# Keeping the turned context of the first cross attention in DRAM for the keys of the second

## The chip, the cores and the metric

The kernel runs on one core of a Trainium2 chip. The metric is the device time of one execution in microseconds (us), of which the median of several runs is taken. A profiled execution gives, beside its own time, a record of each instruction and transfer. The engines are PE (TensorE, matrix products; its weight loads are recorded apart as PEld), DVE (VectorE), ACT (ScalarE), POOL (GpSimd) and SP (SyncE, which here issues transfers). SBUF is the memory on the core that the engines work on; PSUM holds the results of matrix products; DRAM is reached by DMA.

## The reference

A perceiver block with six residual stages: `x` has 16 batches of 64 latents of 256 features, the context has 16 batches of 1024 tokens of 256 features.

```python
x = x + L0_xattn(layernorm(x), ctx_1024)      # first cross attention, raw context
x = x + L0_attn(layernorm(x))
x = x + L0_ffn(layernorm(x))
x = x + L1_xattn(ctx_1024, layernorm(x))      # second cross attention
x = x + L1_attn(layernorm(x))
x = x + L1_ffn(layernorm(x))                  # routed experts
```

The second cross attention matters here. It normalises the context itself, with a gain and a shift, and turns the keys by a rotary embedding over the token's position:

```python
xn = (x - mean(x)) * rsqrt(var(x) + EPS) * gamma_x + beta_x
k_x, v_x = split(xn @ Wkv)           # 8 heads of 64
k_x = k_x * cos + neg_half(k_x) * sin
sim = q @ concat(k_x, k_l).T
out = (softmax(sim) @ concat(v_x, v_l)) @ Wo
```

`k_l` and `v_l` come from the 64 latents of the batch. All arithmetic is in float32.

## The kernel before

**Three stages.** Everything is in one program. The first stage (main loop at L697, 128 steps) does the first cross attention, 16 batches by 8 pairs of heads; the small stages after it (self attention and feed-forward, `small_stages` L307) are cut into pieces and woven in between. The second (main loop at L1434, 64 steps, from about 1153 us to 1982 us) does the second cross attention, with the self attention and the routing of the last stage woven in. The third runs the experts.

**First stage.** A batch's context is loaded in two halves of 512 tokens (`load_ctx` L216, 512 KB each, issued on SP into the pool of context buffers). The scores need the context with features on the partitions: `turn_context` (L552) turns it with transposes on DVE and 16 copies from SBUF to SBUF into `ctxT[b]`, two buffers of 128 x 2 x 1024 elements. The first batch is turned on PE (`first_context` L540). The tokens of `ctxT` stand in blocks: the index is (a, k, s), token 128 k + 32 a + s. `context_stats` (L571) gathers mean and variance of each token into `cstat`. Softmax probabilities are turned by one DVE transpose (`x_pb`, L606) and 16 copies on SP (`x_pT`, L612); the products with the context (`x_po`) take them. `x_out` is the last product of the stage.

**Second stage.** For each half of 512 tokens: `fetch` (L804) loads the raw context again, up to four halves ahead; `normalise` (L809) subtracts the mean and multiplies by 1/std in place, on ACT, a quarter (256 tokens) at a time; `turn_context` (L821) turns a quarter with four transposes on PE (`l_pt`, issued by line 105) and evicts them in two ACT instructions that multiply by the gain (L835) into `l_cnT`. `keys` (L857) makes keys (a "key pair" is two calls of it, for four of the eight heads): four matmuls (`l_pk`), two evictions on ACT with the bias (L877, `l_kr`), a product with cos on DVE (L878), four copies on SP that swap halves (L886, `l_ks`), a product with sin on POOL (L889) and a sum on DVE (L890). `gather` (L1052) multiplies the probabilities with the normalised context not turned (`l_po`); it has one PSUM buffer, emptied on DVE (L1066, `l_pct`). Probabilities are turned as in the first stage (L1019, 16 copies `l_pT` at L1028). `shifts` (L844) makes the bias of keys and values from the layer norm's shift, in 32 narrow matmuls (`l_pb`).

**What orders the work.** In the second stage PE keeps the order in which the program writes its matrix instructions. The other engines' order is set by a scheduler from that text, the dependencies and the buffers. Each engine works its own list in order, so what stands behind a waiting instruction waits too. `weave` (L1407) interleaves keys, turning, the woven pieces (`items`) with the eight products of `gather` for the step (`fill`). At the head of the stage (from L1388) the statistics of the latents, the first normalisations, `shifts`, the first turnings and four key pairs run in the order written, then the main loop starts. All small PSUM results (`l_pt`, `l_pk`, `l_pb` and those of the woven stages) share a pool of three banks.

## Time and profile before

| | |
|---|---|
| runs | 2128.99, 2125.99 and 2124.79 us, median 2125.99 |
| profiled execution | 2112.25 us, its span from first to last instruction 2110.5 us |
| mean granted TensorE clock | 0.990 |
| busy | PE 2021.1, DVE 1313.3, ACT 816.8, POOL 342.0 us |
| DMA | 225.82 MB, mean 107 GB/s |
| bias of keys (`l_pb`) | 3.68 us, at 1152.96 us |
| turning (`l_pt`, `l_cnT`) | 256 transposes on PE, 128 evictions on ACT |
| sin products (L889) | 128 on POOL, 166.2 us, mean 1319 ns |

How it is read: the profile gives each engine's busy time and the number of its instructions; a table of stretches gives the same for parts of the span, with the granted clock and the busy share of the DMA engines. A group's row names a line, an engine and an operation with its tiles (`out<-in`), the count, and the shortest, median and longest duration in ns. A waits' row names an instruction, what released it, and how long in total, how often and how long at most it waited. The timeline lists groups of instructions by start and duration. A float32 matrix product leaves two records, a transpose one. Many steps share helper lines: 101 is every matmul, 105 every transpose by PE, so tiles tell them apart.

### The profile page before, as it was taken

Reading aid. Unit: us, or ns where it says so; the run is one execution under the profiler, and the core shown is the slowest. Engines: PE = TensorE matmul, PEld = TensorE weight load, DVE = VectorE, ACT = ScalarE, POOL = GpSimd, SP = SyncE. Lnnn points to the kernel's source line nnn. Section 1 sums busy time; section 2 is a strip of 40 time slices with the busy share of each in tenths; the row PEclk is TensorE's granted clock in tenths of the full one; section 3 lists DMA queues with packets and bytes.
Section 4 is the critical chain, followed back from the end, with each engine's and each line's share of the span. In section 5 each row is a group of like instructions: output and inputs, shape, how many; then the busy total and the mean of one; then the engine's idle time right before and its main releaser. Section 6 shows DMA issues by size and latency. Waiting matters only on the chain. (4 is left out here: it accounts for less than half of the span.)

```text
span 2110.5 us, 30756 instructions
## 1 busy us (share of the span) xinstructions
PE 2021.1 (96%) x10906; PEld 1369.8 (65%) x10906; DVE 1313.3 (62%) x2678; ACT 816.8 (39%) x1584; POOL 342.0 (16%) x329
## 2 busy tenths in 40 slices
PE   7899999999999999999998889899999999999988
PEld 4567666666667666666666445566666666666777
DVE  6765656757666567576653666666767676767431
ACT  2323234224333342243343435445555545554231
POOL 3200100001001000010010323222323232323111
PEclk9999999999999999999999999999999999999999
DMA  7344334333343343344433145744444444444443
GB/s 258 86 105 103 74 83 104 98 71 99 85 105 76 83 105 98 71 116 107 109 80 90 42 98 155 202 100 111 108 105 111 109 108 105 107 101 106 132 165 109
DMA packets 159432, 225.82 MB, mean 107 GB/s; under 512 B 36408, under 2 KB 95374, under 8 KB 158768
## 3 DMA queue, kind: packets, MB, share of 16 engines
q1 hardware_dynamic: 153456, 204.12, 38.0%
q0 software_dynamic: 5824, 19.74, 2.8%
q8 instruction: 88, 1.44, 0.3%
q14 instruction: 64, 0.52, 0.1%
HBM read 71.14 MB, written 6.05 MB: 37 GB/s over the span
## 5 line engine op out<-in xcount | busy, mean ns | idle before, releaser
L101 PE MATMUL x_s<-ctxT,x_qk 128*128 128x512 f32 x1024 | 471.2, 601 | 11.5 <-ACT pr_x L597 11.5
L101 PE MATMUL x_po<-x_pT,ctx 128*128 128x256 f32 x2048 | 458.0, 381 | 3.7 <-DMA x_pT<-x_pb 3.7
L101 PEld LDWEIGHTS x_po<-x_pT,ctx 128*128 128x128 f32 x2048 | 387.6, 191 | 79.3 <-issue 26.3
L101 PEld LDWEIGHTS x_s<-ctxT,x_qk 128*128 128x128 f32 x1024 | 187.0, 190 | 211.0 <-issue 181.2
L590 DVE TENSOR_REDUCE nmax_x<-x_s 128x1 f32<-128x1024 f32 x128 | 155.9, 1218 | 238.7 <-PE x_s L101 237.6
L597 ACT ACTIVATE pr_x<-x_s,shift_x 128x1024 f32<-128x1024 f32 x128 | 142.5, 1114 | 287.8 <-DVE shift_x L594 239.5
L101 PE MATMUL l_po<-l_pT,l_ctx 128*128 128x256 f32 x864 | 239.3, 390 | 14.0 <-DMA l_ks<-l_kr 5.8
L101 PE MATMUL l_pk<-l_cnT,wkv 128*128 128x512 f32 x512 | 243.5, 602 | 2.9 <-DVE a_vm L369 1.5
L889 POOL TENSOR_TENSOR l_ks<-l_ks,k 128x512 f32<-128x512 f32 x128 | 166.2, 1319 | 402.3 <-DMA l_ks<-l_kr 338.9
L101 PEld LDWEIGHTS l_po<-l_pT,l_ctx 128*128 128x128 f32 x864 | 154.4, 194 | 83.7 <-issue 61.9
L606 DVE STREAM_TRANSPOSE x_pb<-pr_x 128x1024 f32<-128x1024 f32 x128 | 157.2, 1237 | 6.3 <-DMA x_pT<-x_pb 2.1
L101 PEld LDWEIGHTS l_pk<-l_cnT,wkv 128*128 128x128 f32 x512 | 94.8, 191 | 101.5 <-issue 85.1
L877 ACT ACTIVATE l_kr<-l_pk,l_bkv 128x512 f32<-128x512 f32 x128 | 87.3, 686 | 184.2 <-PE l_pk L101 106.0
L631 ACT COPY x_pct<-x_po 128x512 f32<-128x512 f32 x64 | 37.5, 585 | 244.6 <-PE x_po L101 244.6
L878 DVE TENSOR_TENSOR l_kT<-l_kr,k 128x512 f32<-128x512 f32 x128 | 91.8, 719 | 46.5 <-ACT l_kr L877 46.2
L190 DVE TENSOR_SCALAR pr_x<-pr_x,inv_x 128x1024 f32<-128x1024 f32 x128 | 100.1, 782 | 3.2
L890 DVE TENSOR_TENSOR l_kT<-l_kT,l_ks 128x512 f32<-128x512 f32 x128 | 95.3, 784 | 8.2 <-POOL l_ks L889 8.1
L996 DVE TENSOR_REDUCE nmax_l<-l_s 128x1 f32<-128x1024 f32 x64 | 75.7, 1219 | 33.9 <-PE l_s L101 33.9
L597 ACT ACT_TABLE_LOAD x42 | 53.9, 1283 | 103.9 <-DVE shift_x L594 103.8
L1019 DVE STREAM_TRANSPOSE l_pb<-pr_l 128x1024 f32<-128x1024 f32 x64 | 78.3, 1233 | 4.7 <-DMA l_ks<-l_kr 3.3
L999 ACT ACTIVATE pr_l<-l_s,nmax_l 128x1024 f32<-128x1024 f32 x64 | 71.5, 1118 | 9.8 <-DVE nmax_l L997 9.6
L101 PE MATMUL l_s<-l_kT,l_qT 64*64 64x512 f32 x512 | 66.4, 604 | 4.2 <-DVE l_kT L890 4.2
(307 smaller groups left out, 2598.5 us busy)
## 6 DMA issues: line engine op xcount, KB each, us to landing
x_pT<-x_pb SPq DMA_DIRECT2D x1024, 64.0 KB, 2.0
l_ks<-l_kr SPq DMA_DIRECT2D x256, 128.0 KB, 2.3
l_pT<-l_pb SPq DMA_DIRECT2D x512, 64.0 KB, 2.0
ctx<-in_context_dram SPq DMA_DIRECT2D x32, 512.0 KB, 5.5
w<-in_m_w_dram SPq DMA_DIRECT2D x16, 1024.0 KB, 9.8
ctxT<-x_cb SPq DMA_DIRECT2D x240, 64.0 KB, 2.0
l_ctx<-in_context_dram SPq DMA_DIRECT2D x27, 512.0 KB, 4.5
l_ctx_spare<-in_context_dram SPq DMA_DIRECT2D x5, 512.0 KB
```

What stands on the lines that cost most here:

```text
L101: ins = nc.tensor.matmul(*args, **kwargs)
L190: nc.vector.tensor_scalar(pr, pr, inv, None, ALU.mult)
L590: nc.vector.tensor_reduce(nmax, sc, AX.X, ALU.max, negate=True)
L597: nc.scalar.activation(pr, sc, AF.Exp, bias=shift, scale=1.0, accum_out=total)
L606: nc.vector.transpose(blocks[w][:, :, i], pr.rearrange("p (j k s) -> p j k s", j=4, s=32))
L877: nc.scalar.activation(kr[:, i % 2], pk, AF.Identity, bias=bkv[:, i : i + 1])
L878: nc.vector.tensor_tensor(kr2, kr[:, i % 2], k4[:, 0, at], ALU.mult)
L889: nc.gpsimd.tensor_tensor(ks[:, i % 2], ks[:, i % 2], k4[:, 1, at], ALU.mult)
L890: nc.vector.tensor_tensor(kr2, kr2, ks[:, i % 2], ALU.add)
L996: nc.vector.tensor_reduce(nmax, sc[h], AX.X, ALU.max, negate=True)
L999: nc.scalar.activation(pr[h], sc[h], AF.Exp, bias=nmax, scale=1.0, accum_out=total[:, 2 * h : 2 * h + 1])
L1019: nc.vector.transpose(blocks[w][:, :, h].rearrange("p j k s -> p k j s"), pr[h].rearrange("p (k j s) -> p k j s", k=NKT, s=32),)
```

## The change

The first stage already turns the raw context. Its result is now written to DRAM (`keep_turned`, two transfers of 512 KB a batch, on SP) and read by the second stage in place of the turning there (`load_turned`, 512 KB for each half). The raw turned context is not yet normalised. Three things take the place of that: the gain and the mean are taken into the weights of the keys (`gain_weights`, `center_weights`: each column of the weights gets its mean over the features subtracted, found with a product with ones); 1/std of each token, which now lies along the free axis, is written to DRAM as rows (`store_rstd`), read back to all partitions (`load_rstd`, 256 KB for each half) and multiplied in on POOL (`scale_turned`). `shifts` moves into the first stage's last steps. The PE transposes and ACT evictions of the second stage go.

The raw context is still loaded and normalised for `gather`, from four fixed buffers, one step ahead of its normalisation. Since the turned tokens are in blocks (a, k, s), the table of cos and sin, and the way that the probabilities are turned, follow that order. At the head of the second stage the order of key pairs and woven pieces is written anew, with four key pairs ahead of the first scores. The constant of ones, before part of a loaded table, is filled by POOL at the start.

```diff
+    def keep_turned(b, c):
+        if c == 0:
+            turned[b] = mdram.tile([P, NC, N], F32, tag=f"turned{b}", name=f"turned_{b}")
+        nc.sync.dma_start(
+            out=turned[b][:, c], in_=ctxT[b][:, c].rearrange("p a k s -> p (a k s)")
+        )
...
+    def load_turned(hh, slot):
+
+        b, n = divmod(hh, 2)
+        cn[hh] = slot.rearrange("p t d -> p (t d)").rearrange("p (c m) -> p c m", c=NC)
+        nc.sync.dma_start(out=cn[hh], in_=turned[b][:, :, n * 512 : (n + 1) * 512])
+
+    def store_rstd():
+
+        pt = bank([P, P], "l_rt")
+        transpose(pt, crstd, ident)
+        stage = slots[1][:, 0, 0:P]
+        nc.vector.tensor_copy(stage, pt)
+        for a in range(4):
+            nc.gpsimd.dma_start(
+                out=rstd_rows[:, a], in_=stage[:, 32 * a : 32 * a + 32]
+            )
...
+    def load_rstd(hh):
+        b, n = divmod(hh, 2)
+        row = rstd_rows.rearrange("b a k s -> b (a k s)")[b : b + 1, n * 512 : (n + 1) * 512]
+        nc.sync.dma_start(out=row_of(hh), in_=row.broadcast_to([P, 512]))
+
+    def scale_turned(hh):
+        nc.gpsimd.tensor_tensor(
+            cn[hh], cn[hh], row_of(hh).unsqueeze(1).broadcast_to([P, NC, 512]), ALU.mult
+        )
+
+    def gain_weights():
...
+            nc.scalar.activation(
+                w[:, c, :], wkv4[:, c, 0:512], AF.Copy, scale=cols[:, C_GX + c : C_GX + c + 1]
+            )
+        return w
+
+    def center_weights(w, pm, c):
+        nc.vector.scalar_tensor_tensor(w[:, c, :], pm, -1.0 / D, w[:, c, :], ALU.mult, ALU.add)
...
+        if i == 6:
+            keep_turned(b, 0)
+        if i == 0 and b:
+            keep_turned(b - 1, 1)
...
+        if s == NSTEP - 5:
+            store_rstd()
+            wkc = gain_weights()
+        elif s == NSTEP - 4:
+            pm = bank([P, 512], "l_wm")
+            for c in range(NC):
+                matmul(pm, lhsT=ones, rhs=wkc[:, c, :], start=(c == 0), stop=(c == NC - 1))
+            center_weights(wkc, pm, 0)
+            center_weights(wkc, pm, 1)
+            for hh in range(2):
+                load_rstd(hh)
+        elif s == NSTEP - 3:
+            shifts()
+        elif s == NSTEP - 2:
+            for hh in range(2):
+                scale_turned(hh)
...
+        raw_slots = [slots[4], slots[5], slots[0], slots[2]]
+
         def fetch(hh):
-            if hh not in raw and hh < NHALF:
-                b, h = divmod(hh, 2)
-                raw[hh] = load_half(cpool, b, h, "l_ctx", spare[:, 0] if hh % 7 == 3 else None)
+            if hh < NHALF:
+                raw[hh] = load_half(None, hh // 2, hh % 2, "l_ctx", raw_slots[hh % 4])
...
-        def turn_context(qq):
...
+        def next_turned(hh):
+            if hh < NHALF:
+                slot = spare[:, 0]
+                if hh % 3 != 1:
+                    slot = two.tile([P, 4, D], F32, tag="cnT", name=f"l_cnT_{hh}")
+                load_turned(hh, slot)
+                load_rstd(hh)
...
-                        pk, lhsT=wkv4[:, c, i * P : (i + 1) * P], rhs=cnT[hh][:, c, :],
+                        pk, lhsT=wkc[:, c, i * P : (i + 1) * P], rhs=cn[hh][:, c, :],
...
             nc.vector.transpose(
-                blocks[w][:, :, h].rearrange("p j k s -> p k j s"),
-                pr[h].rearrange("p (k j s) -> p k j s", k=NKT, s=32),
+                blocks[w][:, :, h], pr[h].rearrange("p (j k s) -> p j k s", j=4, s=32)
             )
...
+        for hh in range(2):
+            next_turned(hh + 2)
+            fetch(hh)
+        latent_stats(0)
+        latents(0)
         key_pair(0)
         issue_one()
         key_pair(2)
-        turn_context(4)
-        turn_context(5)
+        turn_latents(0)
+        queries(0)
         issue_one()
         key_pair(1)
+        issue_one()
+        key_pair(3)
         scores(0)
         soften(0, 0)
-        issue_one()
-        key_pair(3)
-        turn_context(6)
+        scale_turned(2)
+        next_turned(4)
         issue_one()
         key_pair(4)
+        for qq in range(2):
+            normalise(qq)
         for s in range(NSTEP):
             t, at = divmod(s, PER_TILE)
             if s % 2 == 0:
-                fetch((s + 8) // 2)
+                fetch((s + 2) // 2)
             elif s + 1 < NSTEP:
                 scores((s + 1) // 2)
             turn_probs(s)
             if s + 1 < NSTEP:
                 soften((s + 1) // 2, (s + 1) % 2)
-            normalise(s + 7)
+            if s % 2:
+                normalise(s + 1)
+                normalise(s + 2)
+                next_turned((s + 9) // 2)
+            elif (s + 6) // 2 < NHALF:
+                scale_turned((s + 6) // 2)
             items = [lambda j=j: keys(s + 5, j) for j in range(2)]
-            items.append(lambda: turn_context(s + 7))
```

## The prediction

> **What bounds the kernel now.** I read the totals first, then the table of busy time by stretch, then the groups of the changed lines, then the waits, and for single costs the timeline.
>
> ```profile
> PE 2021.1 (96%) x10906; PEld 1369.8 (65%) x10906; DVE 1313.3 (62%) x2678; ACT 816.8 (39%) x1584; POOL 342.0 (16%) x329
> ```
>
> TensorE (PE) is the bound over the whole span: work taken off it shortens the kernel unless another engine turns late. The stretches (columns: window, PE, PEld, DVE, ACT, POOL busy, clock, DMA share, GB/s) show where this holds less well:
>
> ```profile
> 1153.00:1170.00 17.00, 15.15 (x93) 12.77 (x92) 4.65 (x14) 11.00 (x26) 1.64 (x2) 0.80 0.21 75
> 1170.00:1190.00 20.00, 14.90 (x71) 7.99 (x69) 9.87 (x16) 8.06 (x17) 10.36 (x9) 1.00 0.23 52
> 1190.00:1240.00 50.00, 37.64 (x157) 18.13 (x161) 37.37 (x62) 19.30 (x42) 15.25 (x12) 0.90 0.34 81
> 1300.00:1500.00 200.00, 187.87 (x1092) 124.88 (x1093) 134.45 (x254) 94.49 (x202) 53.19 (x47) 0.98 0.52 138
> ```
>
> From 1153 us the second cross attention starts up: PE is idle for 87 - 67.7 = 19.3 us until 1240. After that it is 94 to 98% busy. So there are two regimes: a start that is a chain of dependent steps, and a steady part in which PE time is the time.
>
> **The change, part by part.** *Removed: the turning of the normalised context.* 64 quarters, each with 4 PE transposes, 2 ScalarE evictions and a PSUM bank.
>
> ```profile
> L105 PE MATMUL l_pt<-ident,l_ctx x216: 272/273/456, 1156.5 to 1885.5; 128*128 128x128 f32 x108
> L835 ACT ACTIVATE l_cnT<-l_pt,cols x128: 458/474/512, 1157.6 to 1916.8; 128x256 f32<-128x256 f32 x128
> L878 DVE TENSOR_TENSOR l_kT<-l_kr,k x128: 639/686/1540, 1169.4 to 1934.0; 128x512 f32<-128x512 f32 x128
> ```
> ```profile
> L270 POOL TENSOR_TENSOR x_prod<-wq,rowsb x2: 2347/2360/2372, 14.5 to 44.9; 128x1024 f32<-128x1024 f32 x2
> ```
> ```profile
> 1510.31 0.60 PE L105 MATMUL l_pt<-ident,l_ctx 128*128 128x128 f32 x4
> ...
> 1510.75 1.03 PE L101 MATMUL l_po<-l_pT,l_ctx 128*128 128x256 f32 x4
> ...
> 1516.22 2.49 POOL L889 TENSOR_TENSOR l_ks<-l_ks,k 128x512 f32<-128x512 f32 x2 [1.46 <-DMA l_ks<-l_kr]
> ...
> 1517.72 1.54 DVE L878 TENSOR_TENSOR l_kT<-l_kr,k 128x512 f32<-128x512 f32 x1 [0.22 <-ACT l_kr L877]
> ```
>
> The transpose row's 0.273 us each is not what one displaces, since matmuls overlap: 256 x 0.273 = 70 us is too much. In the timeline the next group starts 0.44 us after a group of four, so a quarter costs 0.44 us, 64 of them 28 us. The union of their busy spans (0.60 us, 64 times) gives 38 us as the other end. I take 0.43, being start to start in a full PE. 16 of the 64 quarters fall into the start-up and the steps just after it; the other 48 are worth 48 x 0.43 = **-20.6 us** (to -28 at the 0.60 of the busy spans). ScalarE loses 128 x 0.474 = 61 us; at 39% busy this is worth nothing itself, but l_k evictions find ScalarE and the three PSUM banks free sooner.
>
> *Start-up.* Now the first key matmul (l_pk) waits for normalised context, turned, evicted, and for the 32 narrow matmuls of the bias (l_pb):
>
> ```profile
> 1152.96 3.68 PE L101 MATMUL l_pb<-cols,wkv 128*128 128x1 f32 x32
> 1156.50 1.95 PE L105 MATMUL l_pt<-ident,l_ctx 128*128 128x128 f32 x8
> ...
> 1166.76 3.60 PE L101 MATMUL l_pk<-l_cnT,wkv 128*128 128x512 f32 x8
> ...
> 1187.79 1.09 PE L101 MATMUL l_s<-l_kT,l_qT 64*64 64x512 f32 x8
> ```
>
> With the change the turned keys of two halves lie ready, scaled, before 1153, so l_pk starts there. Ahead of the first scores go 3.68 (l_pb) and 1.95 + 1.91 + 1.04 = 4.9 us of transposes; one more key pair (3.6) is put ahead of them, out of what followed. The idle of 1.85 us at 1160, for the latents' statistics, is covered by l_pk. The pair is work that later steps no longer do, so 3.7 + 4.9 = 8.6 us is what the start gains if nothing else changes. I take **-8 us**, with ends -2 (the sin/cos chain through four copies, POOL and DVE becomes the limit; new waits, below) and -14 (its idle goes too).
>
> *Added on PE, in the first stage:* the bias (3.68 us by its row, only moved), two 128x512 ones-matmuls for the mean (the l_pk row has four of that size, two records each, in 3.60 us: 1.8) and one transpose of 1/std (0.1), in a stretch where PE is full (18.89 of 23.00 us before 1153): **+5.5**. ScalarE's two gains of weights, DVE's two centrings of 128x512 and the POOL copies of 1/std lie beside it. A `ones` fill put early on POOL delays the first weight load: **+0.5**.
>
> *Added on DMA.* First stage: 32 writes of 512 KB on SP. Their cost lies between 0 and what they delay. A 512 KB load took
>
> ```profile
> l_ks<-l_kr SPq DMA_DIRECT2D x256, 128.0 KB, 2.3
> ...
> l_ctx<-in_context_dram SPq DMA_DIRECT2D x27, 512.0 KB, 4.5
> ```
>
> 4.5 us to land against 2.0 for a 64 KB x_pT, so about 2.5 us behind each. They stand ahead of batches of 16 x_pT copies, mostly one or two, late in the stage up to four together: 4 x 2.5 = 10 us. The x_pT copies have 3 to 15 us from the last issue to first use (2.0 of it landing), and SP was idle 5 to 9 us before those batches. Four or so places could lose up to 3 us: 0 to 12; I take **+1**. Second stage: each half (512 tokens, 25 us) issues a turned load of 512 KB and a 256 KB broadcast of 1/std on SP, 27 issues where there were 25. The DMA share was 0.43 to 0.52, and 768 KB more on about 2.7 MB a half leaves room. The raw half now comes one step (11.4 us) before its normalisation instead of several; 4.5 to 5.5 us of landing fits. Should it not, the softmax exponent stands behind it on ScalarE, and scores behind that.
>
> *Added on POOL.* 32 products 128x1024. The nearest row is x_prod, same shape and operation: 2.36 us; 75 us in all. By half: 2.36 us more on an engine that is 27% busy here. It holds no result up while it has three steps (34 us), which it has. What it costs is the port to SBUF. The row: L878 takes 686 ns at the median and up to 1540; the one at 1517.72 took 1.54 us while POOL's pair ran from 1516.22 to 1518.71. The rule: the Trainium skill, "SBUF — State Buffer", section "Who interferes with whom", says whoever issues first gets the shared pair "for the whole instruction; the other **fully blocks**", and that DVE operations with two SBUF inputs count. By the rule at its full price each product may stop DVE for 2.36 us, and 75 us against the gain would make the sum positive (+53). The trace agrees on the blocking but not on the price to PE: in 1300 to 1880 POOL's l_ks products already hold 51 pairs x 2.5 = 128 us, while PE's whole idle, of every cause, is 21 us. So at most 16% of it reaches PE: 75 x 0.16 = 12. With l_pct, which frees the single buffer l_po, among DVE's blockable operations, I take **+3** for ports and queues, ends 0 and 12.
>
> *No cost:* the probabilities transposed in another order (DVE's 128x1024 transposes took 1233 ns in one order in L1019 and 1237 in the other in L606).
>
> **Sum:** -20.6 - 8 + 5.5 + 0.5 + 1 + 3 = **-18.6 us**. Against the profiled execution, 2112.25 us (span 2110.5, the rest around it), that is 2093.7. The runs' median is 13.7 us higher; a saved PE microsecond is the same in both, so 2125.99 - 18.6 = **2107.4 us**. Ends by the same terms: -28 - 14 + 6 = -36, 2090; -20.6 - 2 + 6 + 12 + 12 = +7, 2133. All of the worst together being unlikely, the likeliest's own range is 2092 to 2121.
>
> **Rivals.** (a) *The port takes it back.* For: POOL and DVE overlap already as shown. Against: the 21 us of idle. With +12 to +18 instead of +3 the time is 2116 to 2123, hardly a change.
>
> (b) *The key chain becomes the bound, slower.* A key pair goes ScalarE, SP's four copies, POOL, DVE, then scores.
>
> ```profile
> POOL l_ks L889 <- DMA l_ks<-l_kr: 338.9, 47, 12.0
> ```
> ```profile
> SPq L886 <- ACT l_kr L877: 70.4, 31, 17.4
> ```
>
> (What was waited for, us in total, times, longest.) POOL's idle already ends on these copies, 47 times. In the trace the chain of a pair has 3.5 to 10.7 us of slack before its scores in the steady part, and none up to about 1355 us. The new load and the broadcast are issued directly ahead of four such copies: 2.5 + 1.3 us by the landing times; and a product on POOL ahead of l_ks 2.4: 6.2 in all. It decides once the delay exceeds 3.5. At the full price (6.2 - 3.5) x 28 halves + 6.2 x 4 = 100 us; if a third of that happens, 2107 + 33 = **2140**. Against: products and loads are issued once a half, two key pairs have 25 us between them, and the three rarely meet.
>
> (c) *The writes in the first stage stall x_po.* 12 to 25 us if each late batch finds its ring full: 2118 to 2132.
>
> (d) *PE has holes where the transposes lay, so that little is gained.* Only in the start-up does the table show such holes; then only the steady 20 us minus costs remain: 2113.
>
> **How the numbers follow.** What a measurement of this kernel can tell from no change is about 0.2%, 4.3 us: 2121.7 to 2130.2. Likeliest, (d) with it, 2092 to 2121: 0.56, all faster. A larger gain, below 2092: 0.05. (a): 0.14, of it 0.05 faster, 0.07 same, 0.02 slower. (b): 0.17, slower. (c): 0.08, of it 0.02 same, 0.06 slower. Faster 0.66, same 0.09, slower 0.25. For 8 in 10: 0.04 lies below 2088, and some 0.11 above 2145, the upper two thirds of (b): **2088 to 2145**.
>
> **What would show it.** Right: no l_pt and l_cnT groups; PE busy down by some 30 us; first l_pk near 1159 (1153 and the 5.5 added before it), first l_s near 1187 with a key pair more done by then, first l_po near 1231 where it was 1233; PE at 94 to 98% in the same stretches; x_po's idle <-DMA near its 3.7. Wrong if l_s or l_pk idles on DVE l_kT or POOL l_ks by tens of us (b), if L878 and L890 have a mean near 0.9 us and l_po waits on l_pct (a), if x_po waits for x_pT by over 15 us (c), or if the first l_po comes later than 1237 (start-up).

## The result and the profile after

The changed kernel takes **2151.09 us** (median of four runs, 2147.68 to 2152.47) where the kernel before took 2125.39 (2124.75 to 2128.99): a ratio of **1.0115** with a 95% interval of 1.0097 to 1.0133. It is 25.7 us slower; 2107.4 was forecast. The profiled execution took 2151.67 us, its span 2149.8 us, at a mean granted clock of 0.975 (0.990 before). The totals, and five groups of instructions (the columns are busy time and mean ns of one, then the idle time of the engine before them and what ended it):

```profile
PE 2022.4 (94%) x10655; PEld 1358.3 (63%) x10655; DVE 1379.8 (64%) x2681; ACT 771.5 (36%) x1458; POOL 431.7 (20%) x366
```
```profile
L103 PE MATMUL x_po<-x_pT,ctx 128*128 128x256 f32 x2048 | 457.6, 381 | 5.8 <-DMA x_pT<-x_pb 5.8
...
L103 PE MATMUL l_po<-l_pT,l_slot 128*128 128x256 f32 x1024 | 280.4, 397 | 27.3 <-DMA l_pT<-l_pb 10.4
...
L948 DVE TENSOR_TENSOR l_kT<-l_kr,k 128x512 f32<-128x512 f32 x128 | 117.0, 918 | 63.2 <-ACT l_kr L947 63.1
...
L960 DVE TENSOR_TENSOR l_kT<-l_kT,l_ks 128x512 f32<-128x512 f32 x128 | 106.8, 874 | 32.8 <-POOL l_ks L959 32.6
...
L103 PE MATMUL l_s<-l_kT,l_qT 64*64 64x512 f32 x512 | 73.6, 621 | 14.1 <-DVE l_kT L960 12.3
```

PE has 251 recorded instructions fewer, and is busy for 1.3 us *more*. What the change adds on PE (two products with ones and one transpose) is small against that, so what remains takes longer. And PE idles more: 27.3 us before `l_po`, 14.1 before `l_s`. `x_po` hardly waits for its transfers (5.8 us), so the writes of the first stage aren't where the time went. L948 and L960, the product with cos and the sum on DVE, are 0.2 and 0.1 us longer than before (719 and 784 ns). The same four stretches as before:

```profile
1153.00:1170.00 17.00, 13.32 (x60) 10.41 (x61) 3.88 (x15) 3.33 (x8) 1.69 (x3) 0.90 0.39 117
1170.00:1190.00 20.00, 15.41 (x75) 10.10 (x74) 11.26 (x18) 7.76 (x17) 11.27 (x8) 0.91 0.62 190
1190.00:1240.00 50.00, 36.14 (x128) 13.61 (x126) 37.81 (x63) 23.99 (x52) 20.31 (x17) 0.90 0.38 98
1300.00:1500.00 200.00, 179.76 (x963) 114.65 (x962) 145.32 (x234) 81.83 (x165) 70.11 (x51) 0.94 0.62 167
```

In 1300 to 1500 PE is busy 179.76 of 200 us where it was 187.87, DVE is busier (145.32 against 134.45), POOL too (70.11 against 53.19), and the clock is 0.94 against 0.98. The steady part shows it best. First the kernel before, then the changed one, one row of 500 us each (PE, PEld, DVE, ACT, POOL busy, clock, DMA share, GB/s):

```profile
1400.00:1900.00 500.00, 489.53 (x3158) 324.95 (x3156) 351.48 (x699) 257.45 (x535) 134.08 (x110) 1.00 0.42 106
```
```profile
1400.00:1900.00 500.00, 468.89 (x2896) 305.62 (x2895) 388.87 (x671) 222.61 (x442) 185.84 (x126) 0.97 0.51 133
```

PE is busy for 20.6 us less of the 500, and at a clock 0.03 lower, which is another 15 us of full-speed work.

**Stage by stage**, from the same traces (us; "steady" runs from the first `l_s` of scores 8 to that of scores 30, 22 of the 32):

| | first stage ends (`x_out`) | from there to scores 8 | steady | rest |
|---|---|---|---|---|
| before | 1153.1 | 233.9 | 552.2 | 171.3 |
| after | 1168.6 | 232.9 | 572.9 | 175.4 |
| forecast of the difference | +7 | -8 and -2.6 (6 quarters by 0.43) | -18.1 (42 quarters by 0.43) | - |

The two profiles differ by 39 us, the medians by 26. The kernel before's profiled execution lies 13 us under its other runs. Two experiments below whose first stage is that of the kernel before (b2, b1) end it at 1158.9 and 1162.0 us, but at a lower granted clock in this stage: 0.993 and 0.990, against 0.997 before and 0.994 after. Each end multiplied by its clock gives 1150 us for all three of these, 1162 for the profile of after, and 1158 to 1162 for the other changed kernels that make all the writes. By this estimate the change costs 8 to 12 us in the first stage. The large surprise is the steady part: 20.7 us longer where 18.1 less was forecast. PE's time in those stretches divides as follows:

| | PE busy | PE idle | sum |
|---|---|---|---|
| before | 541.1 | 10.9 | 552.0 |
| after | 539.0 | 34.0 | 573.0 |

Without the transposes 523.0 us of busy time should be left (541.1 - 18.1). PE is busy for 16.0 us more than that, which is about what the clock of 0.97 takes (0.03 x 573 = 17), and 23.1 us are new idle time; together they make the swing of 39.1. Of the 34.0 idle, 22.3 lie before `s_pt` (the transposes of the self attention's probabilities), 9.0 before `l_po` and only 1.8 before `l_s`.

**One of these stalls.** They come once in each tile of the self attention, about every 104 us, five in this part, of 3.7 to 5.2 us. The trace of the changed kernel around the third (start, duration, engine; in brackets the idle time before, and what ended it), cut where `...` stands:

```profile
1628.72 2.35 POOL L728 TENSOR_TENSOR l_cnT<-l_cnT,l_slot 128x1024 f32<-128x1024 f32 x1 [4.03 <-DMA l_slot<-l_rstd]
...
1634.67 2.45 POOL L1400 TENSOR_TENSOR s_pr<-s_pr,s_sm 128x512 f32<-128x512 f32 x2 [3.60 <-DVE s_sm L1399]
...
1637.08 2.48 POOL L959 TENSOR_TENSOR l_ks<-l_ks,k 128x512 f32<-128x512 f32 x2
...
1638.37 2.34 DVE L960 TENSOR_TENSOR l_kT<-l_kT,l_ks 128x512 f32<-128x512 f32 x2 [2.52 <-POOL l_ks L959]
...
1639.75 0.60 PE L107 MATMUL s_pt<-ident,s_pr 128*128 128x128 f32 x4
...
1640.19 1.03 PE L103 MATMUL l_po<-l_pT,l_slot 128*128 128x256 f32 x4
1640.63 2.34 DVE L1066 TENSOR_REDUCE nmax_l<-l_s 128x1 f32<-128x1024 f32 x2
...
1643.08 1.11 ACT L1069 ACTIVATE pr_l<-l_s,nmax_l 128x1024 f32<-128x1024 f32 x1 [4.44 <-DVE nmax_l L1067]
...
1645.56 0.69 ACT L947 ACTIVATE l_kr<-l_pk,l_bkv 128x512 f32<-128x512 f32 x1
...
1646.39 1.09 PE L107 MATMUL s_pt<-ident,s_pr 128*128 128x128 f32 x4 [5.18 <-ACT l_kr L947]
...
1647.27 1.91 PE L103 MATMUL l_po<-l_pT,l_slot 128*128 128x256 f32 x4
```

Read it from the bottom. The second `s_pt` waits 5.18 us, not for its data (POOL had made `s_pr` by 1637.1) but for one of the three PSUM banks; the bank that comes free last holds an `l_pk`. Its eviction `l_kr` stands on ACT behind the softmax exponents. Those waited 4.44 us for the maxima `nmax_l`, which stand on DVE behind the sum L960. And the sum waited 2.52 us for POOL's `l_ks`, whose copies SP had issued by 1624.2, but which stands on POOL behind the self attention's product `s_pr`. A delay on POOL, on the path of a key that isn't needed for another step, passes through DVE and ACT in their order and ends as a missing PSUM bank.

The product with 1/std stands further up in POOL's list (1628.72), but it does not head this chain: it ended at 1631.1, and POOL then idled 3.60 us until DVE had the sums `s_sm`. In all five stalls POOL waited between them for `s_sm`, 3.4 to 6.4 us. The kernel with the product left out (e3 below) has the last two of these stalls, of 3.7 us each, behind the same wait:

```profile
1739.34 1.31 POOL L1400 TENSOR_TENSOR s_pr<-s_pr,s_sm 128x512 f32<-128x512 f32 x1 [9.57 <-DVE s_sm L1399]
...
1751.56 1.02 PE L107 MATMUL s_pt<-ident,s_pr 128*128 128x128 f32 x4 [3.73 <-POOL l_ks L959]
```

After the third stall `s_pt` takes 1.09 us instead of 0.60 and `l_po` 1.91 instead of 1.03. The granted clock of that stretch (PE, PEld, DVE, ACT, POOL busy, clock, DMA share, GB/s) is 0.50; it is 1.00 from 1636 to 1643.4 and again from 1650.2 to 1660:

```profile
1643.40:1650.20 6.80, 3.81 (x10) 2.93 (x11) 5.76 (x11) 3.73 (x10) 3.01 (x2) 0.50 0.49 118
```

**Where POOL and SP wait.** From the chain of waits after (what was waited for, us in total, times, longest), POOL and DVE, then SP:

```profile
POOL l_cnT L728 <- DMA l_slot<-l_rstd: 132.9, 16, 12.4
POOL l_ks L959 <- DMA l_ks<-l_kr: 123.7, 25, 8.1
...
DVE l_kT L960 <- POOL l_ks L959: 32.6, 17, 2.8
```
```profile
SPq L956 <- DVE l_kT L960: 154.2, 37, 9.0
```

The last row is SP's copies waiting for the one buffer `l_ks`, which the sum of the pair before them frees. SP issues in its own order. In a stretch of the steady part it stood thus before, and after:

```profile
1568.37 2.64 SPq L886 DMA_DIRECT2D l_ks<-l_kr  x4
1571.12 0.52 SPq L210 DMA_DIRECT2D l_ctx<-in_context_dram  x1
1577.22 3.67 SPq L1028 DMA_DIRECT2D l_pT<-l_pb  x6
1581.81 2.42 SPq L886 DMA_DIRECT2D l_ks<-l_kr  x4
1584.27 6.30 SPq L1028 DMA_DIRECT2D l_pT<-l_pb  x10
```
```profile
1584.44 2.41 SPq L956 DMA_DIRECT2D l_ks<-l_kr  x4
1586.90 8.19 SPq L1097 DMA_DIRECT2D l_pT<-l_pb  x13
1595.19 0.58 SPq L706 DMA_DIRECT2D l_ctx_spare<-turned  x1
1595.81 0.61 SPq L725 DMA_DIRECT2D l_slot<-l_rstd  x1
1596.52 2.41 SPq L956 DMA_DIRECT2D l_ks<-l_kr  x4
```

Before, the copies of the pair made in an even step (1581.81) went out between six and ten of the 16 `l_pT`. After, they wait for the buffer and go out between three and 13 (1584.44), and the odd step's pair (1596.52) stands behind the 13 `l_pT`, the load and the row. From the end of a pair's second `l_kr` eviction to its first copy it took 0.03 us before for the pairs whose copies SP waited for, and 2.8 at most; after, 3.4 to 7.6 with one exception. From the first `l_pk` to the last sum, the chain of the pair needed soonest (every fourth, made in an odd step) took 14 to 18 us before, with 3.5 to 10.7 to spare ahead of its scores, and 24 to 30 after, with -0.5 to 2.7 to spare.

### The profile page after: what moved, and what is told of

It is laid out like the page before. It is cut to its first block, busy times and chain, and to the rows that moved or that the text cites. A ratio compares the mean times of both kernels' runs of the same rounds, so it can differ in the third digit from the quotient of the medians.

```text
span 2149.8 us, 30317 instructions
## 1 busy us (share of the span) xinstructions
PE 2022.4 (94%) x10655; PEld 1358.3 (63%) x10655; DVE 1379.8 (64%) x2681; ACT 771.5 (36%) x1458; POOL 431.7 (20%) x366
## 5 line engine op out<-in xcount | busy, mean ns | idle before, releaser
L103 PE MATMUL l_po<-l_pT,l_slot 128*128 128x256 f32 x1024 | 280.4, 397 | 27.3 <-DMA l_pT<-l_pb 10.4
L103 PEld LDWEIGHTS l_po<-l_pT,l_slot 128*128 128x128 f32 x1024 | 191.2, 198 | 114.5 <-issue 77.1
L959 POOL TENSOR_TENSOR l_ks<-l_ks,k 128x512 f32<-128x512 f32 x128 | 178.9, 1418 | 190.3 <-DMA l_ks<-l_kr 123.7
L103 PE MATMUL l_pk<-l_cnT,l_slot 128*128 128x512 f32 x320 | 162.9, 637 | 3.6 <-ACT l_kr L947 2.9
L948 DVE TENSOR_TENSOR l_kT<-l_kr,k 128x512 f32<-128x512 f32 x128 | 117.0, 918 | 63.2 <-ACT l_kr L947 63.1
L960 DVE TENSOR_TENSOR l_kT<-l_kT,l_ks 128x512 f32<-128x512 f32 x128 | 106.8, 874 | 32.8 <-POOL l_ks L959 32.6
L103 PEld LDWEIGHTS l_pk<-l_cnT,l_slot 128*128 128x128 f32 x320 | 63.8, 205 | 72.6 <-issue 58.1
L103 PE MATMUL l_s<-l_kT,l_qT 64*64 64x512 f32 x512 | 73.6, 621 | 14.1 <-DVE l_kT L960 12.3
```

Source lines behind the costliest of these rows:

```text
L103: ins = nc.tensor.matmul(*args, **kwargs)
L948: nc.vector.tensor_tensor(kr2, kr[:, i % 2], k4[:, 0, at], ALU.mult)
L959: nc.gpsimd.tensor_tensor(ks[:, i % 2], ks[:, i % 2], k4[:, 1, at], ALU.mult)
L960: nc.vector.tensor_tensor(kr2, kr2, ks[:, i % 2], ALU.add)
```

## The experiments

Ratios are to the kernel before on the same chip in the same session, with the 95% interval. The theories are named as the texts on record name them. A: the product with 1/std sits in a bad place in POOL's list. B: the product itself (its time on POOL, the port). C: the load and the row that SP issues ahead of the copies. D: the place of the copies themselves in SP's list. E: the single buffer `l_ks`. G and H are told in the texts of the last batch.

### Product, row and writes, one by one

```diff
 # e1_scale_in_order
-        nc.gpsimd.tensor_tensor(
+        pin(nc.gpsimd.tensor_tensor(                 # kept in the order of the text
 # e2_no_rstd_load
                 load_turned(hh, slot)
-                load_rstd(hh)
 # e3_no_scale
-        scale_turned(2)
...
-            elif (s + 6) // 2 < NHALF:
-                scale_turned((s + 6) // 2)
 # e5_one_write
-        if i == 6:
+        if i == 6 and b == 0:
             keep_turned(b, 0)
```

> As after, but each product with 1/std keeps its place in the program on POOL, one to two steps later, behind the sin product of the key pair before it, where its row of 1/std has long landed. Theory A (a closed queue: the product stands ahead of the sin product and waits for a row of 1/std issued just before; the sin product, the sum, the next copies on SP and the 13 l_pT copies behind these turn late): POOL's 183 us of waiting for 1/std falls below 40 us, key pairs get over 3 us of slack again and the time falls by 15 to 25 us, to about 2126 to 2136. Theory B (the port: POOL's 75 us more block DVE, in whatever order): the time stays within 5 us of 2151. Theory C (the added bytes crowd the DMA rings): it stays too.

Measured: 2177.22 us, 1.0283 (1.0240 to 1.0325), slower still. The waits show the price: keys then wait for the scaled context itself.

```profile
PEld l_pk L103 <- POOL l_cnT L728: 39.8, 8, 18.6
PE l_pk L103 <- POOL l_cnT L728: 32.9, 6, 17.7
```

Theory A in this form falls (2126 to 2136 was its forecast): the scheduler's place for the product was the better one.

> As after, but the rows of 1/std of the first two halves are used for all (30 broadcasts of 256 KB are left out). Theory A: the product now waits for the turned load alone, issued 0.6 us earlier and no longer shared with the broadcast: a third to a half of the loss in the steady part goes, 2133 to 2143. Theory B: no change, 2148 to 2153. Theory C: 256 of the 1280 KB a half go, 5 us or so, 2146.

Measured: 2164.18 us, 1.0207 (1.0172 to 1.0242). Taking a transfer *out* made it slower by about 0.9% of the time. The copies then stand directly behind a load, and took 3.9 us to land at the median (2.3 in the kernel before). PE's idle time moved to `l_po` (33.4 us). A cost of the row can't explain a loss when it goes; that something else in the order explains it is likely, but not shown.

> As after, but the 30 products with 1/std in the second stage are left out (their loads stay). Theory A and theory B both say that the steady part gains what was forecast, 40 us less than after: 2106 to 2115. Theory C: the loads stay, so most of the loss stays, above 2140.

Measured: 2149.32 us, 1.0133 (1.0098 to 1.0167): no gain at all. The totals of this kernel:

```profile
PE 2020.0 (94%) x10655; PEld 1357.7 (63%) x10655; DVE 1352.2 (63%) x2681; ACT 771.7 (36%) x1458; POOL 353.1 (16%) x336
```

POOL has lost 78.6 us and DVE 27.6 (1379.8 to 1352.2), so the product did lengthen DVE's work by 0.9 us each. The time stayed, and the steady part took 572.2 us (572.9 with it). In this order something else is later still, in the traced stalls the wait for `s_sm`. B alone isn't enough; that the product costs nothing doesn't follow, as the last batch shows.

> As after, but only the first batch's turned context is written and every half reads that (30 of the 32 writes of 512 KB are left out). If the writes stall the first stage by the 4 to 8 us that the start and the last x_po wait suggest, 2143 to 2147; if those come from the order at the start alone, 2149 to 2152.

Measured: 2143.65 us, 1.0113 (1.0077 to 1.0149) with 30 of the 32 writes left out. In its profile the first stage ends 4.1 us earlier than after (1164.5 against 1168.6). The ratios (1.0113 and 1.0115) show no cost of the writes, though their intervals leave room for some 8 us. They aren't the loss.

### SP's order, set by hand

A key pair's copies are put in a function (`rotate`) that may be called later, and SP's transfers are held to the order of the text.

```diff
-            for r in range(4):
...
+            if g == 1 and kk > 4:
+                late.append(lambda: rotate(kk, kr))      # pair of the even step
+            else:
+                rotate(kk, kr)
...
+            while late:
+                late.pop(0)()
```

`e6_odd_first` calls it after the odd pair's copies, with the loads last; `e8_even_first` between the 16 `l_pT` and the odd pair's copies; `e7_loads_last` not at all (text order), with only the loads moved behind the copies. `b1_before_text_order` is the kernel *before*, with nothing but SP held to the order of the text.

> As after, but SP's order in the second stage is fixed by hand: in each odd step the 16 l_pT copies, then the four copies of the odd step's key pair (whose scores come soonest), then those of the even step's pair (12 to 15 us of slack in after), and only then the turned load, the row of 1/std and the raw load. Theory D (SP's order: an even pair's copies stand in front of 13 l_pT copies and wait for the one l_ks buffer, and the odd pair's copies stand behind these and behind the loads): the odd pair's copies start at once after its eviction, the chain shortens by 5 to 9 us and the time falls by 20 to 35 us, 2116 to 2131. Theory B (the port on DVE): under 5 us, 2146 or more. Theory C (the loads' bytes delay whatever lands beside them): under 8 us, above 2143.

Measured: 2237.82 us, 1.0568 (1.0549 to 1.0588). The copies of both pairs come in a row and share the one buffer, so PE waits for keys outright:

```profile
PEld l_s L103 <- DVE l_kT L979: 131.9, 37, 9.3
PE l_s L103 <- DVE l_kT L979: 109.8, 17, 8.4
```

> As after, with SP's order fixed by hand as the text of the kernel has it, but the turned load and the row of 1/std behind the odd pair's copies in place of ahead of them. All 16 l_pT copies then stand behind the even pair's. Theory D: the wait stays, only the 1.3 us of issue and some 2.8 us of landing go, against three more copies (1.9 us) ahead: 2140 to 2153. Theory C: the loads no longer sit in front of copies, 25 us less: 2120 to 2130.

Measured: 2163.53 us, 1.0228 (1.0198 to 1.0258). Moving the loads behind the copies doesn't help while the copies stand behind all 16 `l_pT`: C by itself (2120 to 2130) falls in this order. D's 2140 to 2153 is missed too, as are its ranges for e6 and e8.

> As e6_odd_first, but the even step's copies ahead of the odd step's, both behind the 16 l_pT copies. The odd pair's copies then wait for the even pair's sum, as there is one l_ks buffer (2.4 of issue, 2 landing, 2.5 product, 2 to 4 sum after l_pT's end). Theory D: it lies between, 2130 to 2148, and above e6_odd_first. Theories B and C: within 4 us of e6_odd_first.

Measured: 2247.29 us, 1.0619 (1.0597 to 1.0640). The even pair first is as bad: the copies of both pairs again come in a row. PE's wait for keys stays (72.6 us of `l_s` on the sum), and the next `l_pT`, which stand behind the row of copies, come late (24.7 us of `l_po` on them).

> The kernel before, with SP's order in the second stage fixed by hand as its text has it: raw load, even pair's copies, all 16 l_pT copies, odd pair's copies. Nothing else of the change. Theory D: SP's order alone takes the slack of the key pairs (3.5 to 10.7 us) away, and the time rises by 10 to 30 us, to 2130 to 2150. Theories B and C, in which the new product or the new bytes are needed: within 5 us of before.

Measured: 2136.11 us, 1.0088 (1.0068 to 1.0108). The order of SP's transfers alone, without one instruction of the change, costs **18.7 us**. In its profile PE idles 21.2 us in the steady part, where it was 10.9. D holds here: the place of the copies moves the time. All three of my orders for the changed kernel were worse than the one that they should mend.

### The order of before, given back

`f2_split` sets the even pair's copies in the middle of the 16 `l_pT`, and loads last, near to what the scheduler had made before (six ahead and ten behind, as the trace above shows). `b2_before_split` gives that order to the kernel before. `f4_split_scale` also pins the product. `a0_after_again` is the changed kernel once more, on the same chip.

```diff
+                        if w and 4 * a + j == 8:
+                            while late:
+                                late.pop(0)()
                         ins = nc.sync.dma_start(
                             out=pT[w][32 * j : 32 * j + 32, a], in_=pb[32 * a : 32 * a + 32, j]
```

> The changed kernel itself, on the chip of the next three: 1.0115 times before, about 2142 where before takes 2118.

> As e7_loads_last (odd pair's copies, turned load, row of 1/std, raw load), but the even pair's copies stand in the middle of the 16 l_pT copies, eight ahead and eight behind, near to the order that the kernel before has (10 and 6). Nothing is left out. Theory D: the even pair's copies no longer wait, since the odd pair's sum is done when eight l_pT copies are out; the odd pair's start within 2 us of its eviction: 25 to 40 us less than e7_loads_last, 2122 to 2137. Theory B or C (product and bytes are all there): at most 8 us less, over 2152.

> As f2_split, and from the fifth half on the product with 1/std keeps its place in the text on POOL, behind the odd pair's sin products. If the product ahead of these and its wait for the row are still on the chain: 5 to 20 us less than f2_split; if SP alone was: within 4 us of it.

> The kernel before with the same order on SP as f2_split has (no turned loads): eight l_pT copies, even pair, eight l_pT copies, odd pair, raw load. Theory D: as fast as before, 0.998 to 1.003 of it, against 1.0088 with the 16 copies behind the even pair.

Measured: 2147.69 us, 1.0136 (1.0106 to 1.0165) for the changed kernel again; **2137.02**, 1.0078 (1.0051 to 1.0106) for the split order; 2149.80, 1.0138 (1.0110 to 1.0166) with the product pinned; 2126.06, 1.0038 (1.0028 to 1.0047) for the kernel before in the split order. So the order gives back 10.7 us, and isn't quite as good for the kernel before as its own. It moves the loads as well as the copies, and the runs don't divide the 10.7. Nor does it give the keys their slack back: the chain of the pair needed soonest takes 19 to 26 us in f2, and ends 1.4 us after to 1.8 us before its first scores start. Pinning the product (f4) costs 12.8 us, which neither of its expectations allowed. Between the two kernels in this same order 11 us of loss remain.

### Two buffers for the swapped keys

`h1_two_ks` gives the odd pairs a second `l_ks` buffer and takes one from the turned halves, which are therefore loaded a step later; `h2_late_loads` has the later loads alone; `h3_two_ks_loads_last` is h1 with the loads behind the copies.

```diff
+            if kk % 2:
+                ks = spare[:, 0].rearrange("p t d -> p (t d)").rearrange("p (i m) -> p i m", i=2)
+            else:
                 ks = one.tile([P, 2, 512], F32, tag="ks", name=f"l_ks_{kk}")
...
-                next_turned((s + 9) // 2)
+                next_turned((s + 7) // 2)
```

> As after, with a second l_ks buffer, in the place of the third buffer of turned context, whose loads are one step later for that. Nothing is left out. Theory E (the key pairs queue for the one l_ks buffer): held time no longer adds up to the period, even pairs wait for nothing, the stretch from the 8th to the 30th scores falls from 571 to 535 to 552 us, and the time to 2108 to 2130. Theory B or C (port, bytes): under 6 us gained, over 2140.

> The control of h1_two_ks: two buffers of turned context and the later loads, but one l_ks buffer. Theory E: as after, 2140 to 2155, or a little slower, since the products with 1/std have a step less. If the later loads alone made h1_two_ks faster, this is as fast.

> As h1_two_ks, with the turned load and the row of 1/std behind the odd pair's copies on SP. Theory E with the loads' place as a second part: 3 to 12 us less than h1_two_ks, about 2105 to 2120. If the loads' place does not matter once pairs no longer queue: within 3 us of it.

Measured: 2161.61, 1.0183 (1.0166 to 1.0200); 2154.05, 1.0143 (1.0115 to 1.0172); 2141.25, 1.0089 (1.0059 to 1.0119). Counted from its first copy to the end of its sum, the one buffer is taken some 80% of the time before and 94% after, yet a second one makes the kernel slower: E falls. From h1 to h3, which differ in the place of the loads (and of the rows) alone, lie 20.4 us: with two buffers C's place does matter, though e7 showed nothing of it. In h3 every other chain of the pairs needed soonest is back at 17 to 20 us, with up to 5 to spare; the others take 27 to 29 with none. Yet of the 44.2 us that PE idles in the steady part only 2.0 lie before `l_s`: the keys' own lateness is not what PE waits for.

### Product and row left out of the repaired order

f2's order, without the 30 steady products, without the 30 rows, and without both:

```diff
 # f5_split_no_scale, f7_split_neither
-        scale_turned(2)
...
-            elif (s + 6) // 2 < NHALF:
-                scale_turned((s + 6) // 2)
 # f6_split_no_row, f7_split_neither
-                load_rstd(hh)
```

> The split order of SP, and the 30 products with 1/std of the steady part are left out (the keys are then not scaled). Theory G (once SP's order is repaired, what is still lost comes from the work put in front of the l_ks products: here POOL's 2.36 us product and its waits): 2120 to 2130 us, PE idle over w8 to w30 back under 20 us. Theory H (what is still lost comes from elsewhere, from the few late bank and l_pct releases behind ACT's and DVE's own queues, and the slower clock after each): within 5 us of the split order's 2137.

> The split order of SP, and the 30 steady transfers of the row of 1/std are left out (the product takes what stands in the buffer). Theory G: the product no longer waits for its row, so POOL is free earlier: 2125 to 2135 us. Theory H: within 5 us of 2137.

> The split order of SP with neither the 30 products nor the 30 rows; only the turned halves are loaded. Theory G: the saved transposes show, 2105 to 2118 us, faster than the kernel before. Theory H: still 2128 to 2140 us, no faster than the kernel before; then neither product nor row is what eats the saving.

Measured: f5 **2119.20** us, 1.0011 (0.9997 to 1.0025); f6 2137.25, 1.0110 (1.0081 to 1.0139); f7 2116.39, 1.0002 (0.9988 to 1.0016). Between f6 and f7, which differ by the product alone, lie **20.9 us**; between f5 and f7, by the row alone, 2.8. By ratio f2 to f5, again the product alone, is 0.67%, 14 us; within their intervals the two agree. So the product, whose removal did nothing in e3, has a price in this order. Leaving the row out while the product stays (f2 to f6) gains nothing. The 500 us of the steady part in f2, f5 and f7:

```profile
1400.00:1900.00 500.00, 473.92 (x2948) 309.55 (x2947) 389.00 (x688) 228.67 (x454) 183.42 (x128) 0.98 0.52 135
```
```profile
1400.00:1900.00 500.00, 481.13 (x2991) 318.25 (x2990) 371.72 (x703) 228.76 (x457) 137.94 (x111) 0.98 0.53 139
```
```profile
1400.00:1900.00 500.00, 478.30 (x3023) 315.62 (x3022) 372.74 (x711) 231.37 (x460) 138.27 (x110) 0.99 0.50 129
```

With the product DVE is busy 389 us of 500, without it 372; its instruction counts (688, 703) say that it does slightly less in that time, not more. Theory G holds for the product in the main (f5 came 0.8 us under its range, with 22.0 us of idle where under 20 was named). It misses f6, where H's range holds, and for f7 it doesn't hold either, which was to be 2105 to 2118 *and faster than before*: it is only as fast. The same sums for the steady part:

| | PE busy | PE idle | sum |
|---|---|---|---|
| f2 | 533.9 | 28.6 | 562.5 |
| f6, without the row | 531.5 | 32.0 | 563.5 |
| f5, without the product | 531.6 | 22.0 | 553.6 |
| f7, without both | 525.7 | 24.9 | 550.6 |

The profiled execution of f5 was the slowest of its ten and that of f7 the fastest (13 us apart, where the medians differ by 2.8), so these two rows tell little about the row of 1/std. In f7 the transposes' saving shows at last in PE's busy time (541.1 to 525.7), and is taken by 14 us more idle. 17.4 us of the idle lie before `l_po`, 13.5 of them in a gap of 2.6 to 3.1 us once for each tile of the self attention. The trace of f7 around one of them:

```profile
1696.95 1.28 POOL L1258 DMA_INDIRECT m_norm<-m_x,m_idx  x1 [14.21 <-DVE m_idx L1303]
...
1701.08 0.97 POOL L1258 DMA_INDIRECT out_dram<-xs,m_idx  x1 [0.30 <-issue]
...
1702.07 2.50 POOL L977 TENSOR_TENSOR l_ks<-l_ks,k 128x512 f32<-128x512 f32 x2
...
1703.40 2.34 DVE L978 TENSOR_TENSOR l_kT<-l_kT,l_ks 128x512 f32<-128x512 f32 x2 [3.26 <-POOL l_ks L977]
...
1706.27 0.67 DVE L1158 TENSOR_TENSOR l_pct<-l_po,cols 128x512 f32<-128x512 f32 x1
...
1706.99 1.13 PE L103 MATMUL l_po<-l_pT,l_slot 128*128 128x256 f32 x4 [2.56 <-DVE l_pct L1158]
```

POOL's `l_ks` product stands behind the routing's issues of transfers, the first of which waited 14.21 us for an index from DVE, although the copies that the product needs had been issued by 1690.2. The sum on DVE waits for it, `l_pct` stands behind the sum, and `l_po` has one bank: PE stops for 2.56 us. It is the pattern of the first stall, with the routing in place of the self attention ahead of `l_ks` in POOL's list. In the kernel before the product of that pair began 1.9 us after its last copy was issued.

None of these versions beat the kernel before.

## Why the prediction was wrong

**Where it failed: "Added on POOL" and the +3 "for ports and queues, ends 0 and 12".** I wrote that the product "holds no result up while it has three steps (34 us), which it has". That looked at the product's own result. POOL works in order, and what stands behind the product, the keys' `l_ks` and the sum on DVE, has no such slack. In the split order the product costs 14 us (f2 to f5, by ratio) to 20.9 us (f6 to f7), against ends of 0 and 12. The bound of 16% was worked out from a kernel with 3.5 to 10.7 us to spare in each key chain, and was used for one in which that is gone: 20.9 of the 71 us that 30 products take is 29%. Nor was the whole 2.36 us paid that I had read as the full price from the Trainium skill, "SBUF — State Buffer", section "Who interferes with whom": with the 71 us of products DVE is busy longer by 27.6 us (e3 to after), 33.6 (f5 to f2) and 44.8 (f7 to f6), 0.9 to 1.5 us for each. So rival (a), +12 to +18, had the size. Of its two signs the first was there in the profile of after: L948 and L960 have means of 918 and 874 ns, where 0.9 us was named. It is no proof, as L960 keeps its 884 ns in e3, where no product runs; L948 falls to 790. The second, `l_po` waiting on `l_pct`, came in f2 (16.9 us) and not in after (1.9). How much of the price is the port and how much is POOL's queue the runs don't tell apart; both went with the product.

**What had no term: the place of the copies in SP's list.** I counted the new load and the row as landing times in front of the copies (2.5 + 1.3 us), rival (b), and gave it 0.17 because "the three rarely meet". In the list as it was after the change they stand ahead of the odd step's pair's copies in every half, and with them 13 `l_pT` of 0.63 us each (8.19 us of issuing). b1 shows that such an order costs 18.7 us in a kernel with neither load nor row; f2 shows that 10.7 us come back when it is mended in part. Rival (b) forecast 2140, near the measured time, from the right chain; but it had other transfers as the cause, and it looked for the price in `l_s` idling on `l_kT`, and there it is 12.3 us in all. In the steady part it is 1.8 of 34.0 us of idle; most of it reaches PE elsewhere, as a bank not emptied.

**The two are not a sum.** With SP's order bad, leaving the product out gives nothing (e3). With it good, 14 to 21 us. My table of costs added terms as if each were paid by itself. That they share one slack, so that each is free until the others have used it up, fits e3 and f5, but no run shows the slack itself being used up.

**How much of the miss this covers.** Between forecast and measurement lie 44 us. From the changed kernel to f7, with order, product and row all dealt with, the runs remove 28 (a0 to f7, by ratio). Of the forecast's gain some 20 us are still missing in f7, and for these there is a trace but no experiment (see below).

**What had no term either: the clock.** "PE busy down by some 30 us" came out as +1.3. In the steady part 16.0 us of the loss is slower work. The Trainium skill, "TensorE: Matmul & The Clock Gate", section "HAM oscillation — how this bites in real kernels", warns of PE-idle gaps of more than about 3.4 us; the stalls of the changed kernel are 3.7 to 5.2 us, the granted clock was 0.50 around the third of them, and four `l_po` then take 1.91 us instead of 1.03. In f2 the measurement is stricter than the rule: a gap of 2.56 us was followed by slow `l_po` (796 ns the first, 483 where the clock held), another of 2.66 by none. Counted by its slow matmuls, the stall of 5.2 us costs some 2 us more.

**Point by point.**
- *Transposes, -20.6.* Their work did leave PE: 251 records fewer, and in f7's steady part 15.4 us of busy time less, where -18.1 was worked out and some slow clock is left. The size holds; its gain did not arrive.
- *Start-up, -8.* From `x_out` to scores 8, where -10.6 was forecast, it took 232.9 us against 233.9 in that execution before (240.5 and 242.9 in the two experiments on the kernel before, in other orders of SP). Without product and row (f7) it was 221.3, so the gain is there once order, product and row are dealt with. The first `l_pk` came at 1168.44 where 1159 was named, as the first stage ended late; the first `l_s` at 1198.2 (1187), the first `l_po` at 1243.1 (1231; later than 1237 was a sign of being wrong). Counted from `x_out`, that `l_po` came 5.7 us sooner than before, which was lost again by scores 8.
- *First stage, +5.5 + 0.5 + 1.* 7 in all; 8 to 12 by the estimate above. The first `x_po` started 3.2 us later than in the profile of before (52.7 against 49.5), but no later than in the second experiment on the kernel before (53.0), so the fill of ones isn't seen in it. The writes are 4.1 us of it by e5's profile, nearer to the +1 than to the 12 of rival (c), which falls: `x_po` waited 5.8 us for its transfers.
- *"A saved PE microsecond is the same in both".* The profiled execution of before was 13.7 us faster than the median, and 6 to 9 us of that lie in its first stage if b1 and b2 are the measure. So part of the difference between the profiles is that execution's; it only shifted where the loss seemed to be.
- *Rival (d), holes.* It looked for them in the start-up. They opened in the steady part: f7's PE is busy 15.4 us less there, and the part is 1.6 us shorter.

**What stays open.** In f7 the kernel has its transposes' saving, neither product nor row, and is no faster than before. The trace names POOL's place for the `l_ks` product behind the routing's issues as the start of the regular gap before `l_po`; no run moved it. Nor did a run test the raw load, which the change asks for only one step ahead: ACT waited 38.2 us for it after and 65.6 in f7, where it was some 15 before. e2's loss when a transfer was taken away, and how the product's price divides between port and queue, are open too.

## What to carry to other kernels

Before work is moved from the bound engine to another engine's queue, list what will stand behind the new instructions in that queue, and follow *that* to the bound engine, through every engine that works in order; the slack of the new instruction's own result says nothing about it. Costs on one chain are not to be added or dismissed singly, and an experiment that removes one of them can show nothing while another covers it (e3 and f5 remove the same work, for 0 and for 14 us). When a scheduler makes the order, a change hands it a new problem: run the old kernel in the new order before blaming the new instructions.

## What was not expected of the hardware

A stall of PE costs more than its length: after one of 5.18 us, matmuls ran at nearly half their rate for some 4 us (1.91 us for four `l_po` instead of 1.03), at a granted clock of 0.50, and in the steady part the slower work came to about 16 us beside 23.1 of new idle time. Shorter stalls are enough at times: in f2 and f5 ten of the thirteen gaps of 2.2 to 3.0 us were followed by a stretch at half the clock, in f7 two of six gaps of 2.0 to 3.1. With POOL's product of 2.36 us DVE was busy 0.9 to 1.5 us longer for each. And SP needed some 0.6 us for each issue, so that 13 small transfers in front of four that matter were 8.2 us of SP's time.
